# Routing pieces at other steps of the attention in a fused attention and mixture-of-experts kernel

## The chip, the core and the metric

One Trainium2 chip, one of its cores. The metric is the device time of the whole program in microseconds (us); the kernel before takes 870.91 us (median of 3 runs, 870.66 to 870.98). Durations of single instructions come from one execution taken by the hardware profiler.

## What is computed

Eight batches of 256 rows with 512 columns each. Each batch first goes through cross-attention with 16 heads of width 16 (queries from the normalized rows of `x`, keys and values from `ctx`), then, with the 256 rows of 512 as tokens, through a shared feed-forward block and a router that sends every token to two of eight experts.

```python
x = x + xattn(layernorm(x), ctx, mask, Wq, bq, Wk, bk, Wv, bv)
t = layernorm(x)                                  # (8, 256, 512), tokens
shared  = (sigmoid(t @ sg.T) * (t @ su.T)) @ sd.T
weights = softmax(t @ router_w.T)                 # 8 experts
top_w, top_idx = top_k(weights, 2)
routed  = sum over the two experts of bf16(top_w) * down(sigmoid(gate(t)) * up(t))
x = x + t + shared + routed
```

The experts multiply in bf16, all else is 32-bit. Routing is what the change touches: for each token the two best experts, their weights, and a row number in an expert-sorted table, to which the token's bf16 row and its (place, weight) pair are then scattered.

## The kernel before

**The steps.** The program is written out by hand: the order in which the Python code emits instructions is the order in which each engine's queue runs them. The attention is a loop over 8 batches `b`, 4 head groups `g` in each, and 8 halves `h` in each group (lines 1184 to 1262), so a batch has 32 *steps*, numbered 8g + h, and the program 256. A step emits, in this order:

- `row_max` (L430): two score products on TensorE (L436) for a head group one ahead, then VectorE's maximum of the 1024 scores in each partition (`nm`, L438). The scores have one PSUM buffer, tag s1, so the next step's L436 has to wait for this maximum.
- `exp_scores` (L452): the same products transposed (L459) for the current group, and their exponential on ScalarE (L461).
- on even steps `attend` (L466): probabilities times values (L474).
- at h = 6 `take_max` (L443): four TensorE transposes (L447) and a subtraction on VectorE (L448).
- at fixed steps: `divide` (L491) at steps 2, 9, 18 and 25; `residual` (L516), `token_stats` (L527), `token_norm` (L530, on GpSimd, L535 and L536) and `turn_tokens` (L547, transposes L554) at steps 4 to 7 and 20 to 23; `project_v` (L378, L382) at 21, 23, 25, 27; the next batch's normalization on GpSimd (`start_norm`, L362 and L364) at step 13; on GpSimd also `extra_rows` (L401) at steps 15, 17, 31 and 1; `project_qk` (L404: L411 on TensorE, then two L418 on VectorE) at steps 1, 3, 17, 19.
- last, `plan[8 * g + h]`: whatever the plan of the batch has put at this step.

Since `row_max` comes first in a step, all VectorE work emitted in step n, after its L438, runs before the L438 of step n + 1.

**The plan.** `spread(plan, items, at)` (L1043) puts the items, in order, at the listed steps: so many at each. A batch's plan holds bf16 conversions of the expert weights (`casts`, L321, from GpSimd's queue, at steps 1, 6, 11, 16, 21, 26 of batches 1 to 4), their transposing loads (`turns`, L325 to L329, from SyncE's queue, at steps 3, 8, 13 and so on of batches 2 to 5; every third with a GpSimd memset, L329), routing of the batch before, and the shared feed-forward of the batch before (`SHARED`).

**Routing.** `route(b - 1)` (L564) returns 14 pieces: `logits` (two small transposes L578 and a copy L586), `shift` (L590, L591, and the exponential L592 on ScalarE), `weights` (L596 sum, L597 reciprocal, L598 product), `pick(0)` (L604, L605, L606), `first(0)` (L610, L611, L614), `pick(1)` (L604 to L606), `first(1)` (L610, L611), `share` (L629 to L638), `count` (five small products L646 on TensorE, then L651 and L655), `place` (L659, L661), and four `put` pieces. Each of these converts one row number (L669) and issues two scatters from GpSimd's queue (L195): the token rows to `xs`, the pairs to `whose`. All of routing's other VectorE instructions work on 128 partitions of 2 to 32 elements. In batches 1 to 6, the middle batches of the title, they stand where the changed line puts them; batch 7 has a line of its own (L1201).

Of the kernel before, what the change touches and what calls it, by code (L numbers as in the profile page):

```python
# [36 lines left out]
def xattn_ffn_kernel(  # L37
# [309 lines left out]
    def mask_context(b, engine=nc.gpsimd):  # L347
        s = S[b]
        for i in range(2):
            engine.tensor_mul(s["ctx"][:, i, :], s["ctx"][:, i, :], s["mb"])  # L350
# [79 lines left out]
    def row_max(G, tci, half, tag="s1", later=False):  # L430

        q, k = QK[G]
        ps = ps_s.tile([P, 2, T], F32, tag=tag, name=tag)
        for jj in range(2):
            r = slice(32 * (2 * half + jj), 32 * (2 * half + jj) + 32)
            nc.tensor.matmul(ps[:, jj, :], q[r, tci * P : (tci + 1) * P], k[r, :], start=True, stop=True)  # L436
        c0 = 64 * half + HD * (1 - G % 2) + 2
        best = lambda: nc.vector.reduce_max(NM[G % 2][:, tci, c0 : c0 + 33 : 32], ps, axis=AX.X)  # L438
        if later:
            return best  # L440
        best()

    def take_max(G):  # L443
        q, _ = QK[G]
        ps = ps_m.tile([P, T], F32, tag="mm", name="psn")
        for tci in range(NSTEP):
            nc.tensor.transpose(ps[:, tci * P : (tci + 1) * P], NM[G % 2][:, tci, :], ident)  # L447
        nc.vector.tensor_sub(q, q, ps)  # L448
# [3 lines left out]
    def exp_scores(G, sc, half, tag="s2"):  # L452
        q, k = QK[G]
        if (G, sc) not in ET:
            ET[G, sc] = {}
        ps = ps_s.tile([P, 2, T], F32, tag=tag, name="s2")
        for jj in range(2):
            r = slice(32 * (2 * half + jj), 32 * (2 * half + jj) + 32)
            nc.tensor.matmul(ps[:, jj, :], k[r, sc * P : (sc + 1) * P], q[r, :], start=True, stop=True)  # L459
        e = three.tile([P, 2, T], F32, tag="e", name="e")  # L460
        nc.scalar.activation(e, ps, AF.Exp)  # L461
        ET[G, sc][half] = e
# [3 lines left out]
    def attend(G, sc):  # L466

        b, g = divmod(G, NG)
        V = S[b]["V"]
        if sc == 0:  # L470
            AVT[G] = ps_av.tile([P, T], F32, tag="av", name="av")
        et = ET.pop((G, sc))
        for j in (2, 3, 0, 1):
            nc.tensor.matmul(  # L474
                AVT[G][32 * j : 32 * j + 32, :],
                V[:, sc, 2 * g + j // 2, j % 2 : j % 2 + 2, :].rearrange("p o d -> p (o d)"),
                et[j // 2][:, j % 2, :],
                start=(sc == 0),
                stop=(sc == NSTEP - 1),
            )  # L480
# [3 lines left out]
    def divide_copy(G):  # L484
        u = one.tile([P, T], F32, tag="u", name=f"u{G}")
        nc.scalar.copy(u, AVT.pop(G))
        UT[G] = u
# [42 lines left out]
    def token_norm(b, tt, engine=nc.gpsimd):  # L530
        s = S[b]
        acc = s["acc", tt]
        mv, rs = s.pop(("tstats", tt))
        xn = one.tile([P, T], F32, tag="rd", name="xn")
        engine.tensor_scalar(xn, acc, mv[:, 0:1], rs, ALU.subtract, ALU.mult)  # L535
        engine.tensor_add(acc, acc, xn)  # L536
        s["xn", tt] = xn
# [505 lines left out]
    def spread(plan, items, at):  # L1043
        items = [go for _, go in items]
        for n, count in at:
            while len(plan) <= n:
                plan.append([])
            for _ in range(count):
                plan[n].append(items.pop(0))
        assert not items  # L1050
# [120 lines left out]
    def clear(e):  # L1171

        rows = ROWS if e < E - 1 else ROWS + P
        nc.sync.dma_start(
            out=xs[e * ROWS : e * ROWS + rows, :].rearrange("(n p) t -> p n t", p=P),
            in_=blank.rearrange("p (o t) -> p o t", o=1).to_broadcast([P, rows // P, T]),
        )
        if e == 0:
            nc.sync.dma_start(out=whose.rearrange("(p n) w -> p n w", p=P), in_=nobody)
# [4 lines left out]
    for b in range(B):  # L1184
        plan = later + [[] for _ in range(STEPS - len(later))]
        if b == 0:
            spread(plan, [(1.0, lambda e=e: clear(e)) for e in range(E)], [(16 + 2 * e, 1) for e in range(E)])
            spread(plan, weights, [(11, 1), (13, 1), (15, 1), (27, 1), (29, 1), (31, 1)])
        if 1 <= b <= 4:
            for n in range(6):  # L1190
                plan[5 * n + 1].append(casts.pop(0))
        if 2 <= b <= 5:
            for n in range(6):
                plan[5 * n + 3].append(turns.pop(0))
        if 0 < b:
            short = route(b - 1)
        if 0 < b < B - 1:
            spread(plan, short, [(n, 1) for n in (12, 13, 14, 15, 16, 17, 18, 20, 21, 21, 22, 24, 26, 28)])
            spread(plan, shared_units(b - 1, True), SHARED)
        elif b == B - 1:  # L1200
            spread(plan, short, [(12, 2), (13, 2), (14, 2), (15, 2), (16, 1), (17, 1), (18, 1), (19, 1), (20, 1), (21, 1)])  # L1201
            units = shared_units(b - 1, True)
            spread(plan, units[:24], SOONER)
            units = units[24:]
            sorted_last = route(b, (0,)) + expert_map()
            fetch, whom, experts, weighted, tiles = expert_tiles()
            spread(plan, sorted_last, [(23, 1), (24, 1), (25, 2), (26, 3), (27, 2), (28, 2), (29, 2), (30, 1)])
            plan[30] += [whom, fetch]
        later = plan[STEPS:]
        plan = plan[:STEPS]  # L1210
        for g in range(NG):
            G = NG * b + g
            for h in range(8):
                st, half = divmod(h, 2)

                short = G == 0 and h < 6
                R = 8 * (G + 1) + h + LEAD - short
                if (G or h) and R // 8 < last:
                    row_max(R // 8, (R % 8) // 2, R % 2)
                exp_scores(G, st, half if short else 1 - half, "s2" if R // 8 < last else ("s1", "s2")[h % 2])  # L1220
                if G == 0 and h == 0:
                    row_max(1, 0, 1)
                if half == 0 and st > 0:
                    attend(G, st - 1)
                if G > 0 and h == 0:
                    attend(G - 1, NSTEP - 1)
                    divide_copy(G - 1)
                if h == 8 - LEAD and G + 1 < last:
                    take_max(G + 1)
                if G > 0:  # L1230
                    pb, pg = divmod(G - 1, NG)
                    if h == 1 + pg % 2:
                        divide(G - 1)
                    if pg % 2 == 1:

                        if b == pb == B - 1 and h == 5:
                            token_norm(pb, 0, nc.vector)
                        elif h + (b == pb == B - 1) in FFN:
                            FFN[h + (b == pb == B - 1)](pb, pg // 2)
                if g == 0 and h == 6 and b + 1 < B:  # L1240
                    load_batch(b + 1)
                if g == 1 and h == 0 and b + 1 < B:
                    mask_context(b + 1)
                if g == 1 and h in (2, 3) and b + 1 < B:
                    start_stats(b + 1, h - 2)
                if g == 1 and h == 5 and b + 1 < B:
                    start_norm(b + 1, nc.gpsimd)
                if b == 0 and g == 0 and h in (0, 5, 7):
                    project_v(0, (0, 5, 7).index(h) + 1)
                if (g, h) in V_AT and b + 1 < B:  # L1250
                    project_v(b + 1, V_AT.index((g, h)))
                if g % 2 == 1 and h == 7 and G + 3 < last:
                    extra_rows(G + 3, 0, nc.gpsimd)
                if g % 2 == 0 and h == 1 and G + 2 < last:
                    extra_rows(G + 2, 1, nc.gpsimd)
                if g % 2 == 0 and h in (1, 3) and G + 2 < last:
                    project_qk(G + 2, h // 2)
                for go in plan[8 * g + h]:
                    go()
                if G == 0 and h == 5:  # L1260
                    row_max(1, 3, 1)
                    busy(3, ps_m.tile([P, P], F32, tag="long", name="idle", bufs=1))
# [22 lines left out]
    short = deque(route(B - 1, (1,)) + [(0.0, weighted)])  # L1285
    again, results, adds, own_results = give_back()
    n = 2
# [60 lines left out]
```

## Time and profile before

| | |
|---|---|
| median of 3 runs | 870.91 us |
| profiled execution, its own time | 869.63 us |
| its span, first to last instruction | 867.8 us |
| granted TensorE clock | 1.000 |
| TensorE matmul busy | 826.3 us (95%) |
| VectorE busy | 580.8 us (67%) |
| ScalarE busy | 365.6 us (42%) |
| GpSimd busy | 312.6 us (36%) |

The attention loop makes up most of the span: batches 1 to 6 take 89.5, 89.5, 89.5, 89.5, 90.5 and 89.3 us. The length of a step is the distance in the timeline from its first L459 to that of the next step. In steps 12 to 23, with batch 0 (which has no routing and no shared feed-forward) beside them:

| step | b0 | b1 | b2 | b3 | b4 | b5 | b6 |
|---|---|---|---|---|---|---|---|
| 12 | 2.46 | 2.75 | 2.75 | 2.74 | 2.74 | 2.74 | 2.75 |
| 13 | 2.46 | 2.56 | 2.56 | 2.56 | 2.56 | 2.56 | 2.56 |
| 14 | 2.65 | 2.65 | 2.65 | 2.65 | 2.65 | 2.65 | 2.65 |
| 15 | 2.67 | 3.84 | 2.56 | 2.56 | 2.56 | 4.12 | 2.91 |
| 16 | 2.31 | 2.70 | 2.70 | 2.70 | 2.70 | 2.70 | 2.70 |
| 17 | 2.98 | 2.98 | 2.98 | 2.98 | 2.98 | 2.98 | 2.98 |
| 18 | 2.77 | 3.28 | 3.28 | 3.28 | 3.28 | 3.29 | 3.28 |
| 19 | 2.98 | 2.98 | 2.98 | 2.98 | 2.98 | 2.98 | 2.98 |
| 20 | 2.77 | 2.77 | 2.77 | 2.77 | 2.77 | 2.77 | 2.77 |
| 21 | 2.46 | 2.78 | 2.77 | 2.77 | 2.77 | 2.77 | 2.77 |
| 22 | 2.65 | 2.96 | 2.96 | 2.96 | 2.96 | 2.96 | 2.96 |
| 23 | 2.98 | 3.05 | 3.06 | 3.06 | 3.06 | 2.52 | 2.52 |

How to read it: each step repeats the same instructions to within hundredths of a microsecond from batch to batch, so a step that is longer than another with the same TensorE work is held up by something else. Batch 5 and 6 have no conversions (`casts`), batch 1 and 6 no transposing loads (`turns`).

### The profile page before, as it was taken

Reading aid. Unit: us, or ns where it says so; the run is one execution under the profiler, and the core shown is the slowest. Engines: PE = TensorE matmul, PEld = TensorE weight load, DVE = VectorE, ACT = ScalarE, POOL = GpSimd, SP = SyncE. Lnnn points to the kernel's source line nnn. Section 1 sums busy time; section 2 is a strip of 40 time slices with the busy share of each in tenths; the row PEclk is TensorE's granted clock in tenths of the full one; section 3 lists DMA queues with packets and bytes.
Section 4 is the critical chain, followed back from the end, with each engine's and each line's share of the span. In section 5 each row is a group of like instructions: output and inputs, shape, how many; then the busy total and the mean of one; then the engine's idle time right before and its main releaser. Section 6 shows DMA issues by size and latency. Waiting matters only on the chain.

```text
span 867.8 us, 13410 instructions
## 1 busy us (share of the span) xinstructions
PE 826.3 (95%) x4987; PEld 340.0 (39%) x4987; DVE 580.8 (67%) x1106; ACT 365.6 (42%) x478; POOL 312.6 (36%) x380
## 2 busy tenths in 40 slices
PE   7988989999999999999999999999999989899997
PEld 4322323333333334333433343433343333455573
DVE  7666767776777677867676778676766674543347
ACT  4234444343344334433443343434343445256632
POOL 3114303543354345343525151605251223155520
PEclk9999999999999999999999999999999999999999
DMA  4107962231551257115712350011000000267556
GB/s 159 46 33 239 342 192 78 34 45 43 128 100 30 41 123 122 23 36 123 128 22 42 90 99 1 26 34 52 1 25 13 13 13 25 61 147 170 150 169 242
DMA packets 91973, 75.05 MB, mean 86 GB/s; under 512 B 60321, under 2 KB 77756, under 8 KB 91526
## 3 DMA queue, kind: packets, MB, share of 16 engines
q1 hardware_dynamic: 85302, 53.84, 22.8%
q0 software_dynamic: 5904, 19.70, 10.8%
q8 instruction: 40, 0.66, 0.3%
q10 hardware_dynamic: 704, 0.66, 0.2%
q14 instruction: 23, 0.19, 0.1%
HBM read 37.84 MB, written 40.79 MB: 91 GB/s over the span
## 4 chain that ended last, share of the span: by engine, by line
PE 74%; DVE 19%; issue 3%; POOL 2%; ACT 1%; DMA 0%; DVEq 0%; ACTq 0%; POOLq 0%
PE s L436 24%; DVE nm L438 10%; PE av L474 9%; PE psy L998 5%; PE pu L940 4%; PE psq L411 3%; PE psk L411 3%; PE ey L849 3%; PE eu L820 3%; PE eg L820 3%; PE pgu L940 3%; PE pg L940 3%; DVE q L418 2%; PE s L459 2%; PE psv L378 2%
## 5 line engine op out<-in xcount | busy, mean ns | idle before, releaser
L461 ACT ACTIVATE e<-s 128x1024 f32<-128x1024 f32 x256 | 262.0, 1023 | 398.5 <-PE s L459 396.6
L438 DVE TENSOR_REDUCE nm<-s 128x2 f32<-128x1024 f32 x256 | 313.3, 1224 | 144.4 <-PE s L459 131.3
L436 PE MATMUL s<-k,q 32*128 32x512 f32 x1024 | 287.7, 639 | 25.3 <-DVE nm L438 22.7
L459 PE MATMUL s<-q,k 32*128 32x512 f32 x1024 | 288.5, 640 | 1.5 <-DVE q L448 0.8
L474 PE MATMUL av<-e,V 128*32 128x512 f32 x1024 | 137.4, 605 | 0.2 <-ACT e L461 0.2
L436 PEld LDWEIGHTS s<-k,q 32*128 32x128 f32 x1024 | 76.6, 183 | 130.2 <-DVE nm L438 104.7
L401 POOL TENSOR_SCALAR extra<-mb,alpha,beta 128x512 f32<-128x512 f32 x60 | 45.5, 763 | 146.1 <-DVE q L418 145.7
L343 POOL TENSOR_TENSOR rs<-ve,mhalf 128x1 f32<-128x1 f32 x32 | 18.4, 575 | 217.0 <-DVE ve L341 216.9
L459 PEld LDWEIGHTS s<-q,k 32*128 32x128 f32 x1024 | 76.5, 182 | 5.3 <-issue 4.3
L474 PEld LDWEIGHTS av<-e,V 128*32 128x32 f32 x1024 | 20.3, 108 | 98.2 <-issue 96.3
L195 POOL DMA_INDIRECT xs<-xnb,at x30 | 30.2, 1006 | 73.9 <-DVE at L669 59.3
L826 DVE SCALAR_TENSOR_TENSOR hz<-eth,eu 128x352 bf16<-128x352 f32 x45 | 23.4, 520 | 41.6 <-ACT eth L825 18.2
L998 PE MATMUL psy<-sdT,h 128*128 128x512 f32 (+1 forms) x90 | 45.3, 615 | 0.2 <-issue 0.2
L940 PE MATMUL pu<-xT,sguT 128*128 128x256 f32 x128 | 36.7, 403 | 0.0
L940 PE MATMUL pg<-xT,sguT 128*128 128x256 f32 x128 | 35.3, 401 | 0.0
L378 PE MATMUL psv<-WvT,ctx 128*128 128x256 f32 x128 | 34.8, 394 | 0.0
L940 PE MATMUL pgu<-xT,sguT 128*96 128x256 f32 (+1 forms) x128 | 34.1, 393 | 0.0
L820 PEld LDWEIGHTS <-late_ctx 128*128 128x128 bf16 x296 | 27.6, 98 | 14.0 <-issue 2.6
L411 PE MATMUL psq<-xm,WqT 128*128 128x512 f32 x64 | 32.0, 620 | 0.9 <-DVE xm L1103 0.9
L195 POOL DMA_INDIRECT whose<-who,at x30 | 29.0, 968 | 9.1 <-issue 9.1
L940 PEld LDWEIGHTS pu<-xT,sguT 128*128 128x128 f32 x128 | 21.8, 189 | 25.3 <-issue 22.8
L411 PE MATMUL psk<-ctx,WkT 128*128 128x512 f32 x64 | 31.6, 617 | 0.0
(219 smaller groups left out, 980.4 us busy)
## 6 DMA issues: line engine op xcount, KB each, us to landing
xs<-blank SPq DMA_DIRECT2D x7, 1920.0 KB
x<-in_x_dram SPq DMA_DIRECT2D x7, 512.0 KB
ctx<-in_ctx_dram SPq DMA_DIRECT2D x7, 512.0 KB
accd<-acc SPq DMA_DIRECT2D x12, 256.0 KB
again<-accd POOLq DMA_DIRECT2D x12, 256.0 KB
out_dram<-again SPq DMA_DIRECT2D x12, 256.0 KB
gu<-in_L_ffn_w_gate_dram POOLq DMA_DIRECT2D x8, 352.0 KB
gu<-in_L_ffn_w_up_dram POOLq DMA_DIRECT2D x8, 352.0 KB
```

The costliest lines, as they stand in the source:

```text
L195: i = nc.gpsimd.indirect_dma_start(to[:, :], bass.IndirectOffsetOnAxis(ap=rows, axis=0), what, None, **bounds).ins
L378: nc.tensor.matmul(ps, ct[:, kc, sc * P : (sc + 1) * P], WvT[:, kc, :], start=(kc == 0), stop=(kc == 1))
L401: engine.tensor_scalar(t, S[b]["mb"], at, be, ALU.mult, ALU.add)
L411: nc.tensor.matmul(ps, W[:, kc, g // 2].rearrange("p j a d -> p (j a d)"), rhs[:, kc, :], start=(kc == 0), stop=(kc == 1),)
L436: nc.tensor.matmul(ps[:, jj, :], q[r, tci * P : (tci + 1) * P], k[r, :], start=True, stop=True)
L438: best = lambda: nc.vector.reduce_max(NM[G % 2][:, tci, c0 : c0 + 33 : 32], ps, axis=AX.X)
L459: nc.tensor.matmul(ps[:, jj, :], k[r, sc * P : (sc + 1) * P], q[r, :], start=True, stop=True)
L461: nc.scalar.activation(e, ps, AF.Exp)
L474: nc.tensor.matmul(AVT[G][32 * j : 32 * j + 32, :], V[:, sc, 2 * g + j // 2, j % 2 : j % 2 + 2, :].rearrange("p o d -> p (o d)"), et[j // ...
L820: nc.tensor.matmul(ps, xT[:, kc, :], weights_of(t, GU, I, (m * NKC + kc) * I), start=(kc == 0), stop=(kc == NKC - 1),)
L940: lambda kc=kc: nc.tensor.matmul(ps, sguT[:, m, kc, i0 : i0 + n + more], s["xT"][:, kc, :], start=(kc == 0), stop=(kc == NKC - 1))
L998: nc.tensor.matmul(t["y"], t["h"][:n, ic, tt * P : (tt + 1) * P], sdT[:n, ic, :], start=(ic == 0 and b < B - 1), stop=(ic == 2),)
```

## The change

One list of steps. The order of routing's pieces, their instructions, buffers and queues stay as they are.

```diff
         if 0 < b < B - 1:
-            spread(plan, short, [(n, 1) for n in (12, 13, 14, 15, 16, 17, 18, 20, 21, 21, 22, 24, 26, 28)])
+            spread(plan, short, [(n, 1) for n in (12, 13, 13, 14, 15, 16, 16, 18, 20, 22, 23, 25, 27, 29)])
             spread(plan, shared_units(b - 1, True), SHARED)
```

| piece | step before | step after |
|---|---|---|
| logits, shift | 12, 13 | 12, 13 |
| weights | 14 | 13 |
| pick(0), first(0) | 15, 16 | 14, 15 |
| pick(1), first(1) | 17, 18 | 16, 16 |
| share | 20 | 18 |
| count | 21 | 20 |
| place | 21 | 22 |
| put, four times | 22, 24, 26, 28 | 23, 25, 27, 29 |

## The prediction

> **What bounds the kernel.** I read the costliest groups of the page first, for who waits for whom.
>
> ```profile
> L438 DVE TENSOR_REDUCE nm<-s 128x2 f32<-128x1024 f32 x256 | 313.3, 1224 | 144.4 <-PE s L459 131.3
> ...
> L436 PEld LDWEIGHTS s<-k,q 32*128 32x128 f32 x1024 | 76.6, 183 | 130.2 <-DVE nm L438 104.7
> ```
>
> TensorE is busy 95%, and the engine it waits for is VectorE: the scores L436 of a step wait for the maximum L438 of the step before, since they share one buffer. In the timeline a step has L459 at 0, the maximum from 1.16 to 2.39, the next L436 at 2.46 at the earliest; a step whose other TensorE work is short takes 2.46, others what TensorE needs (2.56 to 3.06). So VectorE work in front of a maximum is free until the maximum starts later than TensorE's length minus 1.3 us (1.23 of the maximum and 0.07 to the next product). Second I read the timeline where a step is longer than its TensorE work. Step 18 of batch 3 (columns: start, duration, engine, line):
>
> ```profile
> 348.23 1.41 DVE L418 SCALAR_TENSOR_TENSOR q<-psq,mine,extra 128x512 f32<-128x512 f32 x2 [0.77 <-PE psq L411]
> 349.55 0.16 DVE L604 TENSOR_REDUCE best<-left 128x2 f32<-128x16 f32 x1
> 349.75 0.17 DVE L605 TENSOR_TENSOR hit<-left,best 128x16 f32<-128x16 f32 x1
> 349.96 0.17 DVE L606 TENSOR_TENSOR hit<-hit,rank 128x16 f32<-128x16 f32 x1
> 350.05 1.22 DVE L438 TENSOR_REDUCE nm<-s 128x2 f32<-128x1024 f32 x1
> ...
> 351.32 0.70 PE L436 MATMUL s<-k,q 32*128 32x512 f32 x2 [0.56 <-DVE nm L438]
> ```
>
> pick(1) stands behind the two L418, the maximum starts at 2.00 instead of 1.49, and the step takes 3.28. Third, the stretches of step 15 that are long in three batches, by VectorE's and GpSimd's timelines. Batch 5:
>
> ```profile
> 516.48 2.50 POOL L364 TENSOR_TENSOR xm<-xm,mb 128x512 f32<-128x512 f32 x2
> 518.92 0.51 POOL L329 MEMSET dT<- 32x512 bf16 x1
> 519.44 2.26 POOL L401 TENSOR_SCALAR extra<-mb,alpha,beta 128x512 f32<-128x512 f32 x3
> ...
> 519.89 1.82 DVE L598 TENSOR_TENSOR w<-w,m 128x16 f32<-128x16 f32 x1
> ...
> 521.64 1.21 DVE L438 TENSOR_REDUCE nm<-s 128x2 f32<-128x1024 f32 x1
> ...
> 522.91 0.70 PE L436 MATMUL s<-k,q 32*128 32x512 f32 x2 [1.49 <-DVE nm L438]
> ```
>
> L598, 0.176 us elsewhere, takes 1.82 and ends with the last of three L401 on GpSimd. The step takes 4.12 instead of 2.56 (+1.56); likewise batch 1 +1.28 and batch 6 +0.35. Batches 2 to 4 escape: there the memset covers 0.75 to 1.26 of the step, L598 starts at 1.10 and is through.
>
> **The change, part by part.** No instruction is added or removed. All figures are relative to a step's start.
>
> *Step 18* loses pick(1). Its maximum then starts at 1.49, as in step 20, which has the same two L418 in front and takes 2.77; so does step 18 of batch 0. Gain 3.28 - 2.77 = 0.51, six batches: **-3.06 us**. Behind it, share comes after divide's four instructions in step 19. Step 3 shows these ending at 0.95; share's five take 0.77 in step 21 and end at 1.63 here, the maximum runs 1.55 to 2.77, the next L436 is ready at 2.84, and TensorE's projection L411 holds the step to 2.98 anyway. Cost 0, cover 0.14.
>
> *Steps 20 to 23.* count's five products cost 0.21 in step 21 (2.77, against 2.56 for step 27 with the same other work). In step 20 they follow L522: 2.65 (step 14, same form) + 0.21 = 2.86 against 2.77, +0.09. Step 21 gets 2.56 (-0.21), step 22 without count and place 2.65, as step 14 (-0.31). But step 23 then waits for something that does not move:
>
> ```profile
> 360.67 0.57 POOL L343 TENSOR_TENSOR rs<-ve,mhalf 128x1 f32<-128x1 f32 x1 [10.82 <-DVE ve L341]
> ...
> 361.67 0.57 POOL L321 DMA_DIRECT2D gu<-in_L_ffn_w_up_dram  x1
> 362.29 2.08 POOL L535 TENSOR_SCALAR xn<-acc,mv,rs 128x512 f32<-128x512 f32 x1
> ...
> 364.42 0.42 PEld L554 LDWEIGHTS pst<-ident,xn 128*128 128x128 f32 x4 [1.29 <-POOL xn L535]
> ```
>
> The transposes L554 wait for GpSimd's xn, which hangs on the statistics of step 21 (L338 to L341). From the start of step 20, L338 starts at 2.77 + 2.40 = 5.17 before, and at 2.86 + 2.56 - 0.26 = 5.16 after: its own place behind the maximum of step 21. So L554 comes at 10.09 before and about 10.05 after. In batches 5 and 6, without L321, xn ends at 9.45 and L554 starts at 9.56 before, at about 9.47 after. Gain 4 x 0.04 + 2 x 0.09: **-0.3 us** of a promised 2.6.
>
> *Weights at step 13.* L592 on ScalarE ends at 0.07 of step 14; L596 follows 0.03 later (as L826 follows L825), then 0.20 each as in step 15: L598 at 0.50. Normally through by 0.68, before the maximum at 1.16, cost 0. GpSimd decides otherwise. [...] L591, of the same form, ran inside L362 in all six middle batches in 0.174 to 0.176, so L362 does not hold it; L350, of L364's form, held L507 of batch 0 to its end (1.025 instead of 0.175). In batches 1 to 4 L362 lasts to 0.95 and L364 starts only then: cost 0 by the row[...]. I take the row. In batches 5 and 6 the first L364 runs 0.34 to 1.61: L598 is held.
>
> *Step 15* now has pick(0) where weights stood: L604 at 0.70, L605 at 0.90, L606 at 1.10, two products with two SBUF inputs instead of one. At a boundary between back-to-back GpSimd instructions the held one got in once (batch 6) and failed three times (once in batch 1, twice in batch 5). Batch 1: L605 gets through at 1.56 and L606 at 2.31, or both at 2.3 to 2.7; maximum at 2.25 to 2.7 against 2.56: 0. Batch 5: step 14 costs +0.21 (L598 ends 1.64) or +1.43 (2.87; the memset follows), and step 15 then +1.3 or +0.4, since GpSimd keeps its own time; about 1.75 in all against 1.56: +0.2. Batch 6 had luck and paid 0.35. It has no memset between L364 and L401: through after the first L364, step 14 +0.21 and step 15 about +1.0; after the second, +1.42 and nothing left; 1.3 in all, **+0.95**. If it fails there too, it waits for the L401: 2.2, 2.9 or 3.7.
>
> *First(0), pick(1), first(1)* stand behind the maxima of steps 15 and 16, end by 0.6 of the next step, maximum at 1.16: cost 0, cover 0.5. *Place* stands behind L448 in step 23, ends at 1.1, inside a step of 3 us: 0. *Puts*: L669 (0.15) goes behind L382, at the latest at 1.34 in step 26, maximum to 2.5 of 2.70: 0. Their eight scatters move on GpSimd's queue behind xnb's conversion L562 and, at step 23, nothing else; the next needed behind them is L401 of step 31, done in step 30 and first read in step 2 of the next batch. SyncE's queue is not passed; no transfer is waited for before the experts run.
>
> Sum: -3.06 - 0.3 + 0.2 + 0.95 = -2.2, bounds -3.4 (nothing held in 14 and 15 beyond today's) and +0.3 (batch 6 failing always), or more by the last rival. It is made on the execution of 869.63 us (span 867.8), which lies 1.3 below the median; I take the difference off the median, rounding to -2.1: **868.8 us**, own range 868.0 to 869.5.
>
> **Rivals.** 0.2% (1.74 us) is what a measurement can tell from no change.
> - Forecast, chance 0.47: 868.8.
> - Batch 6 fails at both boundaries of step 14 and waits for L401: +1.8 to +3.3 instead of +0.95, total -0.1 to -1.4, **870.3**. For it: three of four such boundaries were lost. Chance 0.28.
> - L364 does not hold L598 at all, as L362 does not: step 14 costs nothing, step 15 about as today; **867.5**. Against it: L350. Chance 0.10.
> - Slower: step 15 of batches 2 to 4. L606 starts about 0.01 later than L598 did, and the memset ends 0.15 after it. [...] the three batches join in: maximum after the first L401 (2.02) or the second (2.77), +0.71 or +1.47 each, 3 x = 2.1 to 4.4, from 868.8 to 871.0 to 873.2, say **872.5**. It decides from L606 starting at about 1.2, or from any loss of the 0.15. Against it: L605 in step 18 overlapped the last 0.10 of an L401 unharmed. Chance 0.15.
>
> Faster: 0.8 of the forecast and the third, 0.48. Slower: nearly all of the last and a little of the second, 0.15. Same: 0.37. The range leaves out most of the last alone: 867.4 to 871.3.
>
> **What would show it.** Step 18 at 2.77 in six batches; steps 21 and 22 at about 2.56 and 2.65 and step 23 grown by 0.4; L598 at 0.17 in batches 1 to 4 and over 1 us in 5 and 6; L605 or L606 long in batches 1, 5, 6 alone. It is wrong if step 18 stays above 2.8, if step 23 does not grow, or if products with two SBUF inputs are long in batches 2 to 4.

## The result, and the profile after

The changed kernel takes 879.52 us (median of 4 runs, 878.76 to 880.42) against 870.94 for the kernel before (median of 4): ratio 1.0099, 95% interval 1.0085 to 1.0114. It is slower by 8.6 us, where the forecast was 2.1 us faster. Its profiled execution takes 880.18 us, span 878.4, with a granted TensorE clock of 0.992 instead of 1.000.

On the page of the changed kernel the two rows that were read first have hardly moved:

```profile
L438 DVE TENSOR_REDUCE nm<-s 128x2 f32<-128x1024 f32 x256 | 313.1, 1223 | 138.6 <-PE s L459 125.2
...
L436 PEld LDWEIGHTS s<-k,q 32*128 32x128 f32 x1024 | 76.9, 183 | 132.5 <-DVE nm L438 113.2
```

The waits of L436 for the maximum grew from 104.7 to 113.2 us, though the one in step 18 got shorter. Step by step, the difference of the two profiled executions (distances between the first L459 of neighbouring steps, us) is:

| step | b0 | b1 | b2 | b3 | b4 | b5 | b6 | sum |
|---|---|---|---|---|---|---|---|---|
| 6 | +1.59 | 0 | 0 | 0 | 0 | 0 | 0 | +1.6 |
| 14 | 0 | +2.24 | +2.28 | +2.27 | +2.28 | +0.19 | +0.19 | +9.45 |
| 15 and 16 | 0 | +0.36 | +1.59 | +1.65 | 0 | +0.02 | -0.16 | +3.5 |
| 18 | 0 | -0.50 | -0.50 | -0.50 | -0.50 | -0.50 | -0.50 | -3.0 |
| 21 | 0 | -0.21 | -0.21 | -0.21 | -0.21 | -0.21 | -0.21 | -1.3 |
| 22 | 0 | -0.30 | -0.31 | -0.31 | -0.30 | -0.31 | -0.30 | -1.8 |
| 23 | 0 | +0.42 | +0.42 | +0.42 | +0.43 | +0.37 | +0.36 | +2.4 |

All other steps agree within 0.03; with 0.26 less ahead of the loop this is the 10.6 us between the spans. Step 18 went as forecast (VectorE and TensorE's weight loads, batch 3):

```profile
358.76 1.41 DVE L418 SCALAR_TENSOR_TENSOR q<-psq,mine,extra 128x512 f32<-128x512 f32 x2 [0.77 <-PE psq L411]
360.09 1.22 DVE L438 TENSOR_REDUCE nm<-s 128x2 f32<-128x1024 f32 x1
...
361.36 0.19 PEld L436 LDWEIGHTS s<-k,q 32*128 32x128 f32 x2 [0.29 <-DVE nm L438]
```

With no choice in between, the maximum follows the two L418 at once, and the next product comes 2.78 after the step's start. Step 23, which waits for GpSimd, grew as forecast (GpSimd and weight loads, batch 3):

```profile
371.61 0.57 POOL L321 DMA_DIRECT2D gu<-in_L_ffn_w_up_dram  x1
372.23 2.08 POOL L535 TENSOR_SCALAR xn<-acc,mv,rs 128x512 f32<-128x512 f32 x1
...
374.36 0.20 PEld L554 LDWEIGHTS pst<-ident,xn 128*128 128x128 f32 x2 [1.72 <-POOL xn L535]
```

The wait of L554 was 1.29 and is 1.72. The loss sits in step 14, which runs from 343.77 to 348.70 in batch 3 (GpSimd, VectorE, TensorE):

```profile
340.60 4.14 POOL L362 TENSOR_SCALAR xm<-x,mv,rs 128x512 f32<-128x512 f32 x2
344.72 2.48 POOL L364 TENSOR_TENSOR xm<-xm,mb 128x512 f32<-128x512 f32 x2
347.15 0.51 POOL L329 MEMSET dT<- 32x512 bf16 x1
...
344.27 3.23 DVE L598 TENSOR_TENSOR w<-w,m 128x16 f32<-128x16 f32 x1
347.42 1.21 DVE L438 TENSOR_REDUCE nm<-s 128x2 f32<-128x1024 f32 x1
...
348.68 0.98 PE L436 MATMUL s<-k,q 32*128 32x512 f32 x2 [2.21 <-DVE nm L438]
```

L598 starts at 0.50 of the step, as the prediction has it, would be through at 344.44, and L364 is recorded only from 344.72 on. Yet L598 is held (its record runs on and VectorE does nothing else) through both L364 and 0.3 beyond, for 3.23 us; the maximum behind it starts 2.5 late, and TensorE stands still for 2.21. The same happens in batches 1, 2 and 4. What follows shows in the windows of the same batch: start and end, then the stretch's length, busy time of each engine, and in the third column from the end the granted clock.

```profile
343.77:348.70 4.93, 2.72 (x24) 0.89 (x23) 4.77 (x5) 1.08 (x2) 4.93 (x6) 1.00 0.22 30
348.98:352.39 3.41, 3.41 (x13) 1.57 (x9) 2.32 (x8) 1.02 (x1) 1.48 (x3) 0.50 0.56 106
```

For 3.41 us after the stall the granted clock is 0.50 (second row, third column from the end), so step 15 takes 4.21 instead of 2.56. Such stretches stand at 52.02, 164.66, 256.82 and 348.98, in batches 0, 1, 2 and 3.

### The profile page after: what moved, and what is told of

It is laid out like the page before. It is cut to its first block, busy times and chain, and to the rows that moved or that the text cites. A ratio compares the mean times of both kernels' runs of the same rounds, so it can differ in the third digit from the quotient of the medians.

```text
span 878.4 us, 13403 instructions
## 1 busy us (share of the span) xinstructions
PE 832.4 (95%) x4987; PEld 344.2 (39%) x4987; DVE 594.8 (68%) x1106; ACT 366.1 (42%) x478; POOL 312.9 (36%) x380
## 3 DMA queue, kind: packets, MB, share of 16 engines
q0 software_dynamic: 5904, 19.70, 10.4%
## 4 chain that ended last, share of the span: by engine, by line
PE 70%; DVE 19%; issue 6%; POOL 3%; ACT 1%; DMA 0%; DVEq 0%; ACTq 0%; POOLq 0%
PE s L436 23%; DVE nm L438 11%; PE av L474 8%; PE psy L998 5%; PE pu L940 4%; PE psq L411 4%; PE ey L849 3%; PE eu L820 3%; PE eg L820 3%; PE psk L411 3%; PE pgu L940 3%; DVE q L418 2%; PE psv L378 2%; PE s L459 2%; PE pg L940 2%
## 5 line engine op out<-in xcount | busy, mean ns | idle before, releaser
L436 PE MATMUL s<-k,q 32*128 32x512 f32 x1024 | 289.8, 644 | 28.2 <-DVE nm L438 25.3
L459 PE MATMUL s<-q,k 32*128 32x512 f32 x1024 | 290.7, 644 | 1.5 <-DVE q L448 0.8
L436 PEld LDWEIGHTS s<-k,q 32*128 32x128 f32 x1024 | 76.9, 183 | 132.5 <-DVE nm L438 113.2
L401 POOL TENSOR_SCALAR extra<-mb,alpha,beta 128x512 f32<-128x512 f32 x60 | 45.7, 767 | 142.7 <-DVE q L418 142.2
L459 PEld LDWEIGHTS s<-q,k 32*128 32x128 f32 x1024 | 76.9, 183 | 5.4 <-issue 4.3
L940 PE MATMUL pg<-xT,sguT 128*128 128x256 f32 x128 | 38.1, 427 | 0.0
L940 PEld LDWEIGHTS pg<-xT,sguT 128*128 128x128 f32 x128 | 24.3, 205 | 20.8 <-issue 18.0
```

The lines of the kernel that those rows point to most:

```text
L401: engine.tensor_scalar(t, S[b]["mb"], at, be, ALU.mult, ALU.add)
L940: lambda kc=kc: nc.tensor.matmul(ps, sguT[:, m, kc, i0 : i0 + n + more], s["xT"][:, kc, :], start=(kc == 0), stop=(kc == NKC - 1))
```

## The experiments

**Which part of the change costs it.** Two kernels, the changed one with weights back, and the one before with weights alone moved:

```diff
-(12, 13, 13, 14, 15, 16, 16, 18, 20, 22, 23, 25, 27, 29)   # changed
+(12, 13, 14, 15, 15, 16, 16, 18, 20, 22, 23, 25, 27, 29)   # weights back
-(12, 13, 14, 15, 16, 17, 18, 20, 21, 21, 22, 24, 26, 28)   # before
+(12, 13, 13, 15, 16, 17, 18, 20, 21, 21, 22, 24, 26, 28)   # weights only
```

Theory A puts the loss on L598, held for 3.23 us in step 14, and on the half clock behind it.

> The changed kernel with weights back at step 14 and pick(0), first(0) both at step 15; all else as changed. Theory A ([...] and half clock after the idle TensorE): step 14 at 2.65 in all six batches, L598 in step 15 as before the change (about 1.5, 0.18 x 3, 1.8 and 0.6 us in batches 1 to 6), no half clock, step 18 at 2.78: 870.9 - 3.0 - 0.3 = 867.6, give or take 0.5. Theory B (the loss comes of the other moved pieces: share, count, place or the scatters): 876 or more, step 14 unchanged from the changed kernel or another step long.

> The kernel before with weights alone at step 13. Theory A: L598 over 3 us in batches 1 to 4 and 1.1 in 5 and 6, step 14 at 4.9 (4 x) and 2.85 (2 x), +9.4; step 15 at 2.56 in all, -3.2, since pick(0) stands behind its maximum; up to four windows of half clock at about 1.5 each; step 18 at 3.28: 877 to 883. Theory B: 871.

Weights back: 868.33 against 872.75 for the kernel before on the same chip, ratio 0.9955 (0.9939 to 0.9972). Step 14 is at 2.65 in all batches, step 18 at 2.78, and L598 is held in step 15 again. The gain of 4.4 is more than the 3.3 forecast; steps 15 to 23 of batches 1 to 6 account for 3.0 of it, and the rest was not traced. One step differs from the forecast: in batch 2 L598, behind the memset, lost to the L401 after it (0.97 instead of 0.18 us, step 15 at 3.28), as the fourth rival of the prediction has it for L606. Weights only: 880.77, ratio 1.0098 (1.0080 to 1.0116), with L598 at 3.19, 3.23, 3.22, 3.23, 1.13 and 1.13 us, and the clock halved after the stalls of batches 1 and 2 (mean granted clock of its profiled execution 0.994). Moving weights alone costs as much as the whole change; the other moved pieces, with weights left, are a gain.

The kernel before with the four scatter pairs alone moved:

> The kernel before with the four scatter pairs alone one step later (23, 25, 27, 29). Theory A: no step changes by more than 0.02, the same time as the kernel before of this call within 0.5. Rival (the scatters on GpSimd's queue delay what stands behind them): steps 24 to 31 or 0 to 2 longer, +1 or more.

871.17 against 871.19, ratio 0.9999 (0.9989 to 1.0009); no step of batches 1 to 7 moved by over 0.02. They cost nothing. (Steps 0, 1 and 10 of batch 0, where no routing runs, are 0.62, 0.64 and 0.20 longer in this profiled execution; steps 0 and 1 lie in a window of half clock, of which more below.)

**Is it the second SBUF input.** The changed kernel, with the reciprocal written to PSUM:

```diff
-            ps = ps_m.tile([P, n, E], F32, tag="mm", name="psr")
+            ps = t["psr"] = ps_m.tile([P, n + 1, E], F32, tag="mm", name="psr")
...
-            nc.vector.reciprocal(m, m)
+            if n == 2:
+                total, m = m, t["psr"][:, n, :n].rearrange("p (n o) -> p n o", o=1)
+                nc.vector.reciprocal(m, total)
...
```

> The changed kernel, but L597 writes the reciprocal into PSUM (a spare column of the logits' tile), so that L598 has one SBUF input and one PSUM input. [...] L598 at about 0.18 in all six batches at the same place and time, step 14 at 2.65, no half clock; pick(0) in front of step 15's maximum is still held in batches 1, 5 and 6, about +3: 867.6, give or take 1.5. Rival C (L598 waits for something else, or is held whatever its inputs are): L598 stays over 3 us in batches 1 to 4, 879.

The product at the same place and time, its line now L602 (VectorE's timeline, batch 3):

```profile
337.10 0.17 DVE L602 TENSOR_TENSOR w<-w,psr 128x16 f32<-128x16 f32 x1
337.76 1.23 DVE L438 TENSOR_REDUCE nm<-s 128x2 f32<-128x1024 f32 x1 [0.48 <-PE s L459]
```

0.17 us instead of 3.23, in all six batches (0.170 to 0.172), beside the same two L364; VectorE even waits 0.48 before the maximum. 870.28 against 872.75, ratio 0.9974 (0.9962 to 0.9986). Step 14 is cured, step 15 is not: it takes 4.06, 3.29, 3.30, 3.30, 4.35 and 2.94, because pick(0) now meets the three L401 at their usual place. In batches 2 to 4 that is the slower rival of the prediction, L606 just missing the end of the memset; it was priced at 0.71 a batch and cost 0.72 to 0.74. The run's own forecast, 3.3 us under the kernel before with batches 1, 5 and 6 held, missed these three; 2.5 came of it.

**Who holds it.** The changed kernel without L364, that is, without the mask's product on the normalized rows:

> The changed kernel without L364: the multiplication of the normalized rows by the mask is left out. It separates who holds L598 at 0.5 of step 14 in batches 2 to 4, where L362 then runs to 0.95 and only a memset follows. Theory A1 (L362 holds it[...]): L598 about 0.48 us, ending with L362. Theory A2 (L362 does not hold it[...]): L598 at 0.18. In both step 14 is at 2.65 in batches 2 to 4, and the time lies at 867 to 870.

GpSimd and VectorE in step 14 of batch 3:

```profile
333.08 4.14 POOL L362 TENSOR_SCALAR xm<-x,mv,rs 128x512 f32<-128x512 f32 x2
337.17 0.51 POOL L329 MEMSET dT<- 32x512 bf16 x1
...
336.75 0.19 DVE L598 TENSOR_TENSOR w<-w,m 128x16 f32<-128x16 f32 x1
```

L598 lies wholly inside the second L362 (335.1 to 337.2) and takes 0.182 to 0.186 in batches 2 to 4. L362 does not hold it; L364 does, from ahead of its recorded start. In batches 5 and 6, where without L364 the L401 come here, L598 took 2.60 and 0.64. The time, with that work left out, is 866.22, ratio 0.9925 (0.9907 to 0.9942), a little under the 867 to 870 forecast.

How far ahead, by small maxima put before weights in a list that has logits and shift at step 12 (the list of the second kernel of the next paragraph):

```diff
             w, m = t["w"], sm("m", 1)
+            for _ in range({0: 2, 1: 1, 2: 2, 3: 3}.get(b, 0) if n == 2 else 0):
+                nc.vector.reduce_max(sm("best", 1)[:, :, 0], w, axis=AX.X)
```

> The best list so far (weights at step 13, pick(0) at 15, the rest clear of GpSimd) with 2, 1, 2 and 3 small maxima (0.16 us, one input) put before weights in batches 1 to 4, so that L598 starts at about 0.24, 0.04, 0.24 and 0.44 of step 14; L364 starts at 0.93 to 0.95 there. It brackets how far ahead of its recorded start L364 holds L598. If L364 alone decides[...], as the runs so far have it (held at 0.50, free when it ended 0.33 ahead in batches 5 and 6): free (0.18) in batches 1 to 3, batch 4 on the edge. If L362's last part holds it: over 0.5 us in batch 4 and perhaps in 1 and 3.

The latest of them, in batch 4 (the product's line is now L600):

```profile
421.00 4.14 POOL L362 TENSOR_SCALAR xm<-x,mv,rs 128x512 f32<-128x512 f32 x2
425.11 2.50 POOL L364 TENSOR_TENSOR xm<-xm,mb 128x512 f32<-128x512 f32 x2
...
424.50 0.17 DVE L600 TENSOR_TENSOR w<-w,m 128x16 f32<-128x16 f32 x1
```

All four were free, though each came about 0.1 earlier than I had placed it; this one ended 0.44 before L364's recorded start. With batches 5 and 6 of the lists that follow (free, ended 0.32 ahead) and the changed kernel (held, would have ended 0.28 ahead in batch 3), the hold by an L364 right behind L362 begins about 0.3 us before its record. Whether L364 holds L598 that early or its record comes late, no run tells apart.

L401 shows no such lead. In the kernel without L364, step 15 of batch 3:

```profile
339.75 0.77 POOL L401 TENSOR_SCALAR extra<-mb,alpha,beta 128x512 f32<-128x512 f32 x1
...
339.79 0.18 DVE L605 TENSOR_TENSOR hit<-w,best 128x16 f32<-128x16 f32 x1
340.00 0.55 DVE L606 TENSOR_TENSOR hit<-hit,rank 128x16 f32<-128x16 f32 x1
```

L605 has two SBUF inputs and runs free inside the first 0.2 of this L401, which stands behind a DMA issue; L606, 0.2 later, is held. Behind a memset the edge was at L401's recorded start: L598 of the kernel before was free in batches 2 to 4, where it ended 0.02 after it, and L606 of the run with PSUM was held there, where it would have ended 0.02 to 0.04 after it.

**Out of GpSimd's way.** If that is the cause, routing gains where no product with two SBUF inputs meets L364 or L401:

```diff
-(12, 13, 14, 15, 16, 17, 18, 20, 21, 21, 22, 24, 26, 28)   # before
+(12, 12, 13, 16, 16, 16, 18, 20, 21, 21, 22, 24, 26, 28)   # first
+(12, 12, 13, 15, 16, 16, 16, 18, 20, 22, 23, 25, 27, 29)   # second
```

> The kernel before with logits and shift at step 12, weights at 13, pick(0), first(0) and pick(1) at 16, first(1) at 18, the rest at its old steps: no product with two SBUF inputs falls into GpSimd's L364 and L401. Theory (only L364 and L401 hold such a product, L362 does not): L598 at about 2.4 of step 13, inside the second L362, takes 0.18; steps 14 and 15 at 2.65 and 2.56 in all batches, -3.2; step 18 at 2.78, -3.0; 6 us under the kernel before of the same call. Rival (L362 holds it too, when it comes in the middle): L598 over 1 us in step 13, and step 14 long, no gain or a loss.

> As the last, with the changed kernel's places for share (18), count (20), place (22) and the four scatter pairs (23, 25, 27, 29), and pick(0) at 15, the other three choices at 16. Theory: steps 14, 15, 18 as the last; steps 21 and 22 at 2.56 and 2.65, step 23 grown by 0.4, another -0.3: 6.3 under the kernel before. Rival: the late places for count, place and the scatters cost something that the stalls hid: over the last by 1 us or more.

The first: 864.50 against 871.27, ratio 0.9921 (0.9907 to 0.9935). The row of L598 over the whole run (minimum, median and maximum in ns):

```profile
L598 DVE TENSOR_TENSOR w<-w,m x9: 166/174/175, 159.0 to 761.6; 128x16 f32<-128x16 f32 x7, 128x8 f32<-128x8 f32 x2
```

It runs in the middle of L362 in all six batches, unheld. Steps 14, 15 and 18 are 2.65, 2.56 and 2.78 in each of them. The second: 864.36, ratio 0.9920 (0.9906 to 0.9933), 0.14 less; the two intervals overlap, so the late places of count, place and the scatters are worth no more than the 0.7 that the steps of the traces show (batches 1 to 6 together: 531.65 and 530.96).

**The half clock.** The changed kernel, with the four transposes L447 of step 14 issued four times in batches 1 to 4, into the same tile:

```diff
-        for tci in range(NSTEP):
+        for tci in list(range(NSTEP)) * passes:
...
-                    take_max(G + 1)
+                    take_max(G + 1, 4 if g == 1 and 1 <= b <= 4 else 1)
```

In the changed kernel TensorE stood still for 2.21 us in this step, and the clock was 0.50 for 3.41 us soon after; here it has work for most of the 2.21.

> The changed kernel with TensorE's four transposes of step 14 (L447) issued four times over in batches 1 to 4, so that TensorE works through most of the 2.2 us for which L598 is held. Theory [...]: L598 and step 14 stay as in the changed kernel (over 3 us, 4.9), but no window of half clock follows in batches 1 to 3, granted clock about 0.999 instead of 0.992 to 0.994, and 3 to 5 us less than the changed kernel. Rival (the half clock has another cause, or the extra work comes on top): clock 0.993, time the same or longer.

> The changed kernel once more, beside the others of this call: 8 to 10 us over the kernel before, granted clock 0.992 to 0.995.

Steps 14 and 15 of batch 3 with the extra work, in the windows:

```profile
340.49:345.42 4.93, 4.04 (x36) 2.20 (x35) 4.77 (x5) 1.09 (x2) 4.93 (x6) 1.00 0.44 62
345.42:347.98 2.56, 2.56 (x17) 1.37 (x17) 2.32 (x7) 1.02 (x1) 1.76 (x3) 1.00 0.82 141
```

Step 14 is as long as without it (4.93), TensorE is busy 4.04 of it instead of 2.72, and the clock stays whole: step 15 takes 2.56. 875.78 against 880.29 for the changed kernel beside it (ratios to the kernel before 1.0060, 1.0046 to 1.0074, and 1.0102, 1.0086 to 1.0117). All five runs have a clock of 0.996 to 0.998, all eight of the changed kernel one of 0.992 to 0.994. So 4.5 us of the loss went with the half clock, and here the program got faster by useless work on TensorE.

**What pins step 23.** The second list above, with the conversion of step 21 emitted at 22, behind L535 and L536:

```diff
-                plan[5 * n + 1].append(casts.pop(0))
+                plan[5 * n + 1 + (n == 4)].append(casts.pop(0))
```

> The best list so far with the conversion (L321) of step 21 moved to step 22, behind L535 and L536 in GpSimd's queue. If step 23 is pinned by GpSimd's xn, as forecast: L535 starts about 0.57 earlier, step 23 at 2.90 instead of 3.48 in batches 1 to 4, another 2.3 us, 8.6 to 9 under the kernel before. Rival: step 23 stays at 3.48, or another wait takes its place.

GpSimd and the weight loads in steps 22 and 23 of batch 3:

```profile
357.19 0.52 POOL L370 MEMSET V<- 128x512 f32 x1
357.70 2.08 POOL L535 TENSOR_SCALAR xn<-acc,mv,rs 128x512 f32<-128x512 f32 x1
...
359.83 0.42 PEld L554 LDWEIGHTS pst<-ident,xn 128*128 128x128 f32 x4 [1.13 <-POOL xn L535]
```

L535 follows the memset at once, L554 waits 1.13 instead of 1.72, step 23 takes 2.88 to 2.90 in batches 1 to 4. 860.75 us, ratio 0.9882 (0.9867 to 0.9896): the fastest of all, 10.4 us under the kernel before. That is more than the 8.6 to 9 forecast; against the three runs of the kernel before whose clock was 1.000 (869.54 to 869.76), as this kernel's was (0.999 to 1.000), the difference is about 8.9.

## Why the prediction was wrong

- **Step 18, -3.06:** right, -3.0. Its cover behind it in step 19 held (2.98 before and after).
- **Steps 20 to 23, -0.3:** right in kind: steps 21 and 22 at 2.56 and 2.65, step 23 grown by 0.42 and 0.37. The sum is -0.7, since count's products cost nothing in step 20 (2.77, not 2.86), and the statistics of step 21 came that much sooner. The run with the later conversion shows the pin itself.
- **Weights at step 13, nothing in batches 1 to 4:** this is the step that failed. "In batches 1 to 4 L362 lasts to 0.95 and L364 starts only then: cost 0 by the row", and "I take the row". The row of L591 was read rightly: L362 holds nothing, in six batches and in the run without L364. What was wrong is to take L364's recorded start, 0.45 after that of L598, for the time from which it holds. Behind L362 it held from about 0.3 before its record (L598 was free where it ended 0.32 ahead, held where it would have ended 0.28 ahead), and L598 then lost to both L364. The forecast had no cost there; it was 2.24 to 2.28 a batch. The prediction's own sign of being wrong came true: products with two SBUF inputs were long in batches 2 to 4. In batches 5 and 6 the forecast's better branch, +0.21, came true with 0.19.
- **Step 15, +1.2 with step 14 in batches 5 and 6:** off by details. Batch 5 pays in step 15 what it paid before (4.14, after 4.12), and with step 14 +0.21 (forecast +0.2); batch 6 was lucky again, +0.03 in all instead of +0.95. Batch 1 gains: without half clock its step 15 is 2.62 instead of 3.84, because GpSimd has run ahead during the stall of step 14.
- **The clock:** not in the prediction at all; the granted clock of 0.50 behind the stalls was put at nothing. Steps 15 and 16 of batches 1 to 3 without it sum to -1.2 (from the run with the extra transposes), with it to +3.6: 4.8 us in the profiled execution. Another 1.6, in step 6 of batch 0, is not of the change (see below).
- **The slower rival** had the right kind of cause, at a place (L606 in step 15) that did not bite in the changed kernel but did where step 14 was cured. (The second rival's total, given as -0.1 to -1.4, is by its own terms -3.16 plus 1.8 to 3.3, so +0.1 to -1.4; nothing hangs on it.)

Altogether: -3.0 - 0.7 + 9.45 in step 14 - 1.35 in steps 15 and 16 + 4.8 of half clock + 1.6 in batch 0 - 0.26 ahead of the loop = 10.5 for the profiled execution. The medians differ by 8.6; the 1.6 of batch 0 is probably most of what lies between, since part of the kernel before's runs have such a loss too (in one set, those with a clock of 1.000 take 870.2 to 870.3, those with 0.996 to 0.998 take 871.2 to 872.3).

That half clock in batch 0 goes with the time at which the clock is first recorded as whole (1.00), as far as 13 traces of 12 kernels show, and not with the change; why, they do not show. (In the changed kernel four 128x128 products take 1.06 us ahead of that time, L251, and 0.66 after it, L447.) No routing runs in batch 0. In the three traces whose clock is first whole at 11.06 to 11.40 us (both of the changed kernel, and the first list out of GpSimd's way), a window of half clock falls on step 6. In the five where it is so at 9.81 to 10.12 (among them the kernel with the scatters alone moved), one falls on steps 0 and 1. In the other five, at 8.34 to 8.96, or at 11.96, none follows; the kernel before (8.96) is one of them. So the two profiled executions of the result differ by this too.

## What to carry to other kernels

Before a small VectorE product with two SBUF inputs is moved, look at what GpSimd does at the new place, with a margin for the records' starts (L364 held from 0.3 us ahead, L401 did not), and price a collision at all of GpSimd's back-to-back work, not at its first instruction (L598 took 3.23 us, through both L364). Where the place can't be changed, one operand in PSUM may free the product (here 0.17 us instead of 3.23). Work that is taken out of a chain gains only up to the next wait in that chain (step 23, where L554 waited 1.72 us instead of 1.29), and a stall can cost more than itself: in batches 1 to 3 it left TensorE idle for 55% to 65% of the 3.41 us before the clock fell to 0.50, at up to 1.65 us each.

## What was not expected of the hardware

- GpSimd's two-operand product (L364, L350) and L401, multiply and add with two columns, held a VectorE product with two SBUF inputs: L598 took 3.23 us beside two L364 and 1.82 beside three L401 (0.176 elsewhere), L507 1.025 beside L350 (0.175 elsewhere). L362, subtract and multiply with two columns, never did (0.174 to 0.186 us in all positions tried). Why L362 does not is open. Both L401 and L362 are the same operation in the profile, of 0.76 and 2.07 us. Where an L364 stood behind L362 the hold started about 0.3 us ahead of the record.
- A waiting VectorE product did not always get in between two GpSimd instructions. Between the first and the second L364 L598 lost in all eight cases of batches 1 to 4 that the changed kernel and the one with weights alone show (3.19 to 3.23 us), and got in in all four of batches 5 and 6 (1.13 to 1.14 us, its record ending within 0.03 of the first one's end). The outcome mostly goes with the exact place and comes again from run to run; batch 2 of the kernel with weights back is the exception.
- The half clock did not come at a fixed distance behind the stalls. Its starts in the changed kernel, at 164.66, 256.82 and 348.98, are 92.16 apart (27 times 3.413), while L598 starts at 158.73, 251.50 and 344.27, 92.77 apart. In the 3.41 us just before the half clock TensorE was busy 0.45, 0.35 and 0.35. Counted on from 348.98 in lengths of 3.413, the stall of batch 4 falls into two stretches; the emptier was busy 0.46, and no half clock followed (start and end of a stretch, its length, busy time of TensorE; the clock stands third from the end):

```profile
48.61:52.02 3.41, 2.31 (x12) 0.92 (x15) 2.11 (x4) 0.29 (x1) 0.00 (x0) 1.00 0.00 0
345.57:348.98 3.41, 1.20 (x12) 0.72 (x12) 3.41 (x3) 0.50 (x1) 3.41 (x5) 1.00 0.00 0
437.72:441.13 3.41, 1.58 (x12) 0.50 (x12) 3.41 (x2) 1.02 (x1) 3.41 (x4) 1.00 0.01 2
```

The first line shows that the busy share alone does not decide: this stretch of batch 0 was busy 0.68, and half clock followed in all three traces that have it; stretches of 0.74 to 0.79 just before the half clock on steps 0 and 1 did the same in five, while one of 0.50 in batch 5 of the run with PSUM did not. What the clock goes by stays open.
